# Two recurrent layers, 128 steps: layer 0's input product on two levels of Strassen, with its PSUM banks lent from layer to layer

## The chip, the core and the metric

The kernel runs on one core of one Trainium2 chip. A core has five engines, each with a queue of its own that it works off in order: TensorE (PE: matmuls, and PEld, its weight loads, which overlap them), VectorE (DVE), ScalarE (ACT), GpSimd (POOL) and SyncE (SP, which here only issues DMAs). Matmul results go to PSUM, 8 banks of 128 partitions x 512 float32. The metric is the time of one execution on the device in microseconds (us), lower is better.

## The reference

Two recurrences over the 128 steps of x (batch 128, 128 steps, 512 features), all in float32, with the same initial state:

```
step0(h, z_t):  gate = sigmoid(h @ Wh.T + z_t @ Wz.T + b);  h' = tanh(h * (1 - alpha) + gate * z_t)
x = x + layer0(x)                 # all hidden states of layer 0
step1(h, xw_t): h' = tanh(xw_t + h @ Wh1),   xw = x @ Wx1 + b1
x = x + layer1(x)                 # result, 128 x 128 x 512
```

Per step and layer there are two products of 128 x 512 by 512 x 512: the **state product** with the last state, which is bound to the order of the steps, and the **input product**, which isn't and is made for several steps at once.

## The kernel before

All data lie with the features on the partitions: a step's x is a tile of 128 x 4 x 128 (feature within a block, feature block, batch). Steps go in groups of G = 4. `prepare_x` (VectorE, L151) transposes a loaded x into the group's tile T (`ring`); a residual add on POOL (L353) puts each layer's state into it in place; `finish` (VectorE, L156, then four stores on SP) transposes it back for the output. Each step has two residual adds per layer, one for each half of the features.

**State product** (L295): 16 matmuls of 128 columns, in two halves of two feature blocks, each half with a PSUM bank of its own, ps0 and ps1 (suffix a for layer 0, b for layer 1). A matmul is two records in the profile. Before it, the bank is seeded with the step's part of the input product by a ScalarE copy (L288), onto which the matmuls accumulate. Layer 0's gate (L338), mix (L342, L344 twice) and tanh (L349) follow per half on ScalarE, VectorE, VectorE and ScalarE. Layer 1 has only the tanh (L364). For t < 4 layer 0's input product goes straight into the state's bank (L306), and the gate takes one ACTIVATE per feature block, with the bias (L336).

**Input product** (`products`, L221): one level of Strassen for a group of four steps. Input and weights are cut in 2 x 2 blocks, and 7 block products do the work of 8; a block product is 4 matmuls of 256 columns (two steps). Four of the 7 need sums of input blocks: `add_up` on POOL (L201, L206). Weight combinations are made once. Results are gathered in two PSUM banks per layer (psx and psv): products 1, 6, 7, 4 accumulate one after the other in psx, 5 and 3 in psv, and 2 in psv anew. Between two products the bank's content is kept by ScalarE (L230) or added to a kept one by VectorE (L249) into the tiles c, from which the seeds are taken. A product that accumulates in a bank therefore waits until the read before it is done. The share of a group's 7 products per step is 2, 2, 2, 1 in the order 1, 5 / 6, 3 / 7, 2 / 4, the same for both layers.

**Order.** Layer 1 runs LAG = 8 steps behind layer 0. In step t PE does layer 0's state product of t, layer 1's of t - 8, then the step's block products of both layers. The kernel writes its order out by hand: `at(due, fn, args)` puts every operation in a list with a due time, worked out from STATE = 3.57 us for a state product and PRODUCT = 1.73 us for a block product, and the list, sorted by due time, is the order in which each engine gets its instructions. Due times set the order only; at run time each engine waits for what its next instruction needs, and everything behind that waits too.

Of the kernel before, what the change touches and what calls it, by code (L numbers as in the profile page):

```python
# [13 lines left out]
def kernel(  # L14
# [31 lines left out]

    nc = tc.nc
# [8 lines left out]
    LAG = 2 * G  # L56
# [3 lines left out]
    xpool = ctx.enter_context(tc.tile_pool(name="xpool", bufs=6))  # L60
# [3 lines left out]
    cpool = ctx.enter_context(tc.tile_pool(name="cpool", bufs=2))  # L64
# [10 lines left out]
    STATE, PRODUCT = 3.57, 1.73  # L75
    def share(t):

        g, k = divmod(t, G)
        return (((), (), (), (5, 6)) if g == 0 else ((0, 1), (2, 3), (4, 5), (6,)))[k]

    start, clock = [], 24.3
    for t in range(T + LAG + 4):
        start.append(clock)
        g = t // G
        layers = (t < T) + (t >= LAG)
        groups = (g + 1 < NG) + (1 <= g <= NG)
        busy = STATE * layers + PRODUCT * len(share(t)) * groups + (STATE + 0.6 if t < G - 1 else 0.0)
        clock += max(busy, STATE + (3.0 if t < T else 0.7))
# [83 lines left out]

    class Layer:
        def __init__(self, name, bias):
            self.name, self.bias = name, bias
            self.sums, self.kept, self.bank, self.pre, self.state = {}, {}, {}, {}, {}
            self.w = const.tile([P, C, C, P], F32, tag=f"w{name}", name=f"w{name}")
            self.wh = const.tile([P, C, C, P], F32, tag=f"wh{name}", name=f"wh{name}")
            self.right = {1: self.block(0, 0), 2: self.block(1, 0), 3: self.block(1, 1)}
            for i in (4, 5, 6, 7):  # L180
                self.right[i] = const.tile([P, 2, 2, P], F32, tag=f"w{name}{i}", name=f"w{name}{i}")
# [4 lines left out]
        def combine_weights(self, i, eng):  # L186
            r, b = self.right, self.block
            one, two = {
                5: (b(0, 1), b(0, 0)), 6: (b(1, 1), r[5]), 7: (b(1, 1), b(0, 1)), 4: (b(1, 0), r[6])
            }[i]  # L190
            eng.tensor_tensor(r[i], one, two, ALU.subtract)
# [5 lines left out]
        def add_up(self, g, i):  # L197
            n, a, s = self.name, lambda i, k: self.act(g, i, k), self.sums
            s[g, i] = spool.tile([P, 2, H, P], F32, tag=f"s{n}_{i}", name=f"s{n}_{g}_{i}")
            if i == 1:  # L200
                nc.gpsimd.tensor_tensor(s[g, i], a(1, 0), a(1, 1), ALU.add)  # L201
            else:
                one, two = {
                    2: (s[g, 1], a(0, 0)), 3: (a(0, 0), a(1, 0)), 4: (a(0, 1), s.get((g, 2)))
                }[i]
                nc.gpsimd.tensor_tensor(s[g, i], one, two, ALU.subtract)  # L206

        def left(self, g, i):
            if i in (1, 2, 4):
                return self.act(g, *{1: (0, 0), 2: (0, 1), 4: (1, 1)}[i])  # L210
            return self.sums[g, {5: 1, 6: 2, 7: 3, 3: 4}[i]]

        def multiply(self, g, i, tag, first):
            if first:
                self.bank[tag] = psum.tile(
                    [P, 2, H * P], F32, tag=f"ps{tag}{self.name}", name=f"ps{tag}{self.name}_{g}_{i}"
                )
            ps, a, w = self.bank[tag], self.left(g, i), self.right[i]
            for m in range(2):
                for c in range(2):  # L220
                    nc.tensor.matmul(  # L221
                        ps[:, m], w[:, c, m, :], a[:, c],
                        start=first and m == 0 and c == 0, stop=c == 1, skip_group_check=True,
                    )

        def evacuate(self, dst, tag, half):

            for m in range(2):
                f = 2 * half + m
                nc.scalar.activation(  # L230
                    dst[:, m].rearrange("p h b -> p (h b)"), self.bank[tag][:, m], AF.Identity,
                    bias=self.bias[:, f : f + 1],
                )

        def keep(self, g, i, tag, half):
            s = spool.tile([P, 2, H, P], F32, tag=f"k{self.name}_{i}", name=f"k{self.name}_{g}_{i}")
            self.evacuate(s, tag, half)
            self.kept[i] = s

        def result(self, g, i, half):  # L240
            self.pre[g, i, half] = cpool.tile(
                [P, 2, H, P], F32, tag=f"c{self.name}_{i}{half}", name=f"c{self.name}_{g}_{i}{half}",
                bufs=1 + i,
            )
            return self.pre[g, i, half]

        def add(self, g, i, half, tag, kept):
            flat = lambda s: s.rearrange("p m h b -> p m (h b)")
            nc.vector.tensor_tensor(  # L249
                flat(self.result(g, i, half)), self.bank[tag], flat(self.kept[kept]), ALU.add  # L250
            )

        def last(self, g):
            self.evacuate(self.result(g, 1, 0), "x", 0)

        def products(self, g, places, time):

            if not 0 <= g < NG:
                return time
            order = (  # L260
                (1, "x", True, self.keep, (g, "p1", "x", 0)),
                (5, "v", True, self.keep, (g, "p5", "v", 1)),
                (6, "x", False, self.keep, (g, "u2", "x", 1)),
                (3, "v", False, self.add, (g, 0, 1, "v", "u2")),
                (7, "x", False, self.add, (g, 1, 1, "x", "p5")),
                (2, "v", True, self.add, (g, 0, 0, "v", "p1")),
                (4, "x", False, self.last, (g,)),
            )
            for place in places:
                i, tag, first, fn, args = order[place]  # L270
# [5 lines left out]
        def from_inputs(self, t, half):  # L276
            g, k = divmod(t, G)
            return self.pre[g, k // H, half][:, :, k % H]

        def state_bank(self, t, half):  # L280
            self.state[t, half] = psum.tile(
                [P, 2, P], F32, tag=f"ps{half}{self.name}", name=f"ps{half}{self.name}_{t}"
# [16 lines left out]

        def input_product(self, t):  # L300

            g, k = divmod(t, G)
            ps = [self.state_bank(t, half) for half in range(2)]
            for c in range(C):
                for m in range(C):
                    nc.tensor.matmul(  # L306
                        ps[m // 2][:, m % 2], self.w[:, c, m, :], ring[g][:, c, k],
# [3 lines left out]
    L0, L1 = Layer("a", per_feature[:, 0]), Layer("b", per_feature[:, 2])  # L311
# [16 lines left out]
    def gate0(t, i):  # L328
# [3 lines left out]
        ps = L0.state.pop((t, i))  # L332
        if t < G:
            for m in range(2):
                f = 2 * i + m
                nc.scalar.activation(s0[t][:, f], ps[:, m], AF.Sigmoid, bias=L0.bias[:, f : f + 1])  # L336
        else:
            nc.scalar.activation(s0[t][:, two[i]], ps, AF.Sigmoid)  # L338
# [40 lines left out]
    at(9.0, small_vectors)  # L379
# [9 lines left out]
    for i, time in ((1, 16.2), (2, 17.4), (4, 18.7), (3, 20.0)):  # L389
        at(time, L0.add_up, 1, i)  # L390
    L0.products(1, (0,), 14.4)
    L0.products(1, (1, 2, 3, 4), 17.4)
# [9 lines left out]
    for kc in range(C):  # L402
        at(start[2] + 6.0 + 1.5 * kc, permute_w1, L1.w, "wx", kc)
        at(start[5] + 5.0 + 1.5 * kc, permute_w1, L1.wh, "wh1", kc)
    for n, i in enumerate((5, 6, 7, 4)):
        at(start[3] + 4.5 + 1.3 * n, L1.combine_weights, i, nc.gpsimd)


    for t in range(T + LAG):
        g, k = divmod(t, G)  # L410
        now = start[t]
        if t + 3 * G < T + G and t + 2 * G < T:
            at(now + 0.01, load_x, t + 2 * G)
        if t < T:
            for i in range(2):
# [5 lines left out]
                if t + 1 >= G and t + 1 < T:  # L421
                    due = start[G] - 1.5 + 0.4 * i if t == G - 1 else end + 2.2
                    at(due, L0.seed, t + 1, i)
                at(end + 2.3, residual, t, i, h0)
            now += STATE
# [4 lines left out]
        if u >= 0:  # L430
            for i in range(2):
# [3 lines left out]
                if u + 1 < T:  # L435
                    at(end + 0.5, L1.seed, u + 1, i)
# [3 lines left out]
        now = L0.products(g + 1, share(t), now)  # L440
        now = L1.products(g - 1, share(t), now)
        if t < G:
            at((start[2] + 1.1, start[3] + 0.5, start[3] + 1.2, start[3] + 4.5)[t], prepare_x, t + LAG)
        elif t + LAG < T:
            at(0.45 * start[t] + 0.55 * start[t + 1], prepare_x, t + LAG)
        if k == G - 1:
            a, b, c = start[t + 1], start[t + 2], start[t + 3]
            for i, due0, due1 in (
                (1, a - 0.25 * (a - start[t]), max(a - 0.12 * (a - start[t]), start[t] + STATE + 2.4)),
                (2, a + 0.07 * (b - a), a + 0.2 * (b - a)),  # L450
                (4, a + 0.55 * (b - a), a + 0.65 * (b - a)),
                (3, b + 0.45 * (c - b), b + 0.55 * (c - b)),
            ):
                if g + 2 < NG:
                    at(due0, L0.add_up, g + 2, i)
                if g < NG:
                    at(due1, L1.add_up, g, i)
# [35 lines left out]
```

## Time and profile before

| | |
|---|---|
| time, median of 3 runs | 1719.63 us (1719.26 to 1719.74) |
| the profiled execution | 1719.64 us, of it the profile's span 1717.8 us |
| PE busy | 1695.2 us in 11848 matmul records |
| VectorE, ScalarE, POOL busy | 634.5, 648.4, 684.5 us |
| one group in mid-kernel (852.58 to 905.34 us) | 52.76 us, PE busy in all of it; VectorE 19.27, ScalarE 20.17, POOL 21.14 us |
| granted TensorE clock | 0.999 |
| DMA | mean 43 GB/s |

A line of the timeline has start, duration, engine, line of the kernel, operation, output<-input with a buffer's name, shapes and count; in brackets, how long the engine was idle before it and what ended that. A matmul's end is modelled, so that from the start of one run of matmuls to the start of the next is the time that it took. "Busy" of 1695.2 us is the union of the records.

### The profile page before, as it was taken

The numbers are of one execution on the slowest core, as the hardware profiler recorded it, in microseconds if no ns is written. First come the engines' busy times: TensorE is split into PE (matmuls) and PEld (weight loads), VectorE is DVE, ScalarE is ACT, GpSimd is POOL, SyncE is SP. The second block draws the span as 40 slices with busy tenths as digits, with TensorE's granted clock in tenths as the row PEclk, the third lists the DMA queues.
The fourth block names the chain that finished last, engine by engine and source line by source line (L and its number), as shares of the span: only waits on it lengthen the run. The fifth ranks groups of instructions, "written<-read, shape, count | busy, mean of one in ns | idle before, by whom it ended". The sixth has DMA issues, their size and how long they took to land.

```text
span 1717.8 us, 30477 instructions
## 1 busy us (share of the span) xinstructions
PE 1695.2 (99%) x11848; PEld 1602.1 (93%) x11848; DVE 634.5 (37%) x1234; ACT 648.4 (38%) x1792; POOL 684.5 (40%) x780
## 2 busy tenths in 40 slices
PE   6999999999999999999999999999999999999998
PEld 6899999999999999999999999999999999999998
DVE  5543333333333334333433333333333433333331
ACT  2433333433334333343333344333433333443343
POOL 2543433444334433344343344333443434444343
PEclk9999999999999999999999999999999999999999
DMA  8101112111111121111111111211111112111112
GB/s 172 38 20 43 38 38 50 38 38 43 43 40 38 38 50 38 38 44 43 39 38 42 46 38 38 46 39 40 39 42 45 38 38 45 42 38 33 24 26 50
DMA packets 153199, 73.58 MB, mean 43 GB/s; under 512 B 16801, under 2 KB 151969, under 8 KB 153057
## 3 DMA queue, kind: packets, MB, share of 16 engines
q1 hardware_dynamic: 148992, 69.53, 18.2%
q10 hardware_dynamic: 3840, 1.84, 0.6%
q8 instruction: 95, 1.56, 0.4%
q0 software_dynamic: 224, 0.27, 0.1%
q14 instruction: 48, 0.39, 0.1%
HBM read 38.02 MB, written 33.55 MB: 42 GB/s over the span
## 4 chain that ended last, share of the span: by engine, by line
PE 97%; DMA 1%; DVE 0%; ACT 0%; issue 0%; POOL 0%; ACTq 0%; POOLq 0%; DVEq 0%
PE ps0b L295 13%; PE ps0a L295 13%; PE ps1b L295 13%; PE ps1a L295 13%; PE psxb L221 13%; PE psxa L221 12%; PE psvb L221 10%; PE psva L221 9%; DMA x<-in_x_dram 1%; PE ps1a L306 0%; ACT s L336 0%; PE ps0a L306 0%; DVE s L344 0%; DVE s L342 0%; ACT h L349 0%
## 5 line engine op out<-in xcount | busy, mean ns | idle before, releaser
L353 POOL TENSOR_TENSOR T<-T,h 128x256 f32<-128x256 f32 x512 | 366.4, 726 | 1011.7 <-ACT h L349 975.0
L342 DVE TENSOR_TENSOR s<-s,T 128x256 f32<-128x256 f32 x256 | 162.7, 636 | 495.8 <-ACT s L338 479.3
L295 PEld LDWEIGHTS ps0a<-h,wha 128*128 128x128 f32 x2032 | 246.5, 192 | 8.2 <-ACT ps0a L288 1.8
L295 PE MATMUL ps0a<-h,wha 128*128 128x128 f32 x2032 | 247.4, 275 | 1.4 <-ACT ps0a L288 1.4
L295 PE MATMUL ps0b<-h,whb 128*128 128x128 f32 x2032 | 248.4, 275 | 0.1
L295 PE MATMUL ps1a<-h,wha 128*128 128x128 f32 x2032 | 247.7, 275 | 0.0
L295 PE MATMUL ps1b<-h,whb 128*128 128x128 f32 x2032 | 247.7, 275 | 0.0
L156 DVE STREAM_TRANSPOSE o<-T 128x512 f32<-128x512 f32 x128 | 91.1, 711 | 400.6 <-POOL T L353 400.6
L295 PEld LDWEIGHTS ps0b<-h,whb 128*128 128x128 f32 x2032 | 237.7, 192 | 0.9 <-ACT h L364 0.7
L295 PEld LDWEIGHTS ps1a<-h,wha 128*128 128x128 f32 x2032 | 237.1, 192 | 0.0
L295 PEld LDWEIGHTS ps1b<-h,whb 128*128 128x128 f32 x2032 | 237.1, 192 | 0.0
L349 ACT ACTIVATE h<-s 128x256 f32<-128x256 f32 x256 | 106.7, 417 | 327.4 <-DVE s L344 327.4
L338 ACT ACTIVATE s<-ps0a 128x256 f32<-128x256 f32 x124 | 47.5, 383 | 377.4 <-PE ps0a L295 377.4
L344 DVE SCALAR_TENSOR_TENSOR s<-h,leak,s 128x128 f32<-128x128 f32 x508 | 164.7, 366 | 9.0
L221 PE MATMUL psxb<-sb,wb 128*128 128x256 f32 x512 | 121.0, 379 | 0.0
L221 PE MATMUL psxb<-T,wb 128*128 128x256 f32 x512 | 121.0, 379 | 0.0
L221 PE MATMUL psvb<-sb,wb 128*128 128x256 f32 x512 | 120.9, 379 | 0.0
L221 PE MATMUL psva<-sa,wa 128*128 128x256 f32 x496 | 117.3, 379 | 0.4 <-POOL sa L201 0.4
L221 PE MATMUL psxa<-sa,wa 128*128 128x256 f32 x496 | 117.3, 379 | 0.0
L221 PE MATMUL psxa<-T,wa 128*128 128x256 f32 x496 | 117.3, 379 | 0.0
L221 PEld LDWEIGHTS psvb<-sb,wb 128*128 128x128 f32 x512 | 97.3, 190 | 13.2
L221 PEld LDWEIGHTS psxb<-sb,wb 128*128 128x128 f32 x512 | 97.0, 190 | 13.0
(78 smaller groups left out, 1758.4 us busy)
## 6 DMA issues: line engine op xcount, KB each, us to landing
out_dram<-o SPq DMA_DIRECT2D x510, 64.0 KB, 1.8
x<-in_x_dram SPq DMA_DIRECT2D x502, 64.0 KB, 2.3
wx_in<-in_L_cond_Wx_dram SPq DMA_DIRECT2D x4, 256.0 KB, 4.6
wh_in<-in_L_cond_Wh_dram SPq DMA_DIRECT2D x4, 256.0 KB, 7.1
x<-in_x_dram ACTq DMA_DIRECT2D x10, 64.0 KB, 4.1
wz_in<-in_L_cond_W_dram ACTq DMA_DIRECT2D x2, 256.0 KB, 6.5
wz_in<-in_L_cond_W_dram SPq DMA_DIRECT2D x2, 256.0 KB, 5.9
wh_in<-in_L_cond_W_dram ACTq DMA_DIRECT2D x2, 256.0 KB, 6.3
```

The lines of the kernel that those rows point to most:

```text
L156: nc.vector.transpose(dst.rearrange("p a (c j) -> p c a j", j=S), src.rearrange("p c (a i) -> p c a i", i=S))
L221: nc.tensor.matmul(ps[:, m], w[:, c, m, :], a[:, c], start=first and m == 0 and c == 0, stop=c == 1, skip_group_check=True,)
L295: nc.tensor.matmul(ps[:, m], self.wh[:, c, 2 * half + m, :], h[t - 1][:, c], start=alone and m == 0 and c == 0, stop=c == C - 1, skip_grou ...
L338: nc.scalar.activation(s0[t][:, two[i]], ps, AF.Sigmoid)
L342: nc.vector.tensor_tensor(s[:, two[i]], s[:, two[i]], at_of(t)[:, two[i]], ALU.mult)
L344: nc.vector.scalar_tensor_tensor(s[:, m], h0[t - 1][:, m], leak[:, m : m + 1], s[:, m], ALU.mult, ALU.add)
L349: nc.scalar.activation(h0[t][:, two[i]], s0[t][:, two[i]], AF.Tanh)
L353: nc.gpsimd.tensor_tensor(r, r, h[t][:, two[i]], ALU.add)
```

## The change

**Layer 0 on two levels** (`DeepLayer`). From group 2 on, each of the 7 block products is itself made by Strassen: 7 inner products of one matmul each (128 columns, one 128 x 128 weight block) for the 4 matmuls of 256 columns. 7 x 7 = 49 for 64. The 7 inner results are not combined in PSUM: they lie side by side in two banks (4 and 3), A0 and A1 or B0 and B1, and outer products accumulate onto them as before. Only after the outer combination, in SBUF, are the inner ones combined: `gather`, and then `seed_deep`, whose last addition writes the state's bank, both on VectorE. Inner sums of the inputs, 8 adds of 512 elements per group, go to VectorE (`add_up_inner`), kind 0 from x itself and kind 1 from POOL's outer sums. Inner combinations of the weights are made once on POOL. Layer 1 and group 1 of layer 0 stay on one level.

**Banks.** The four product banks belong to no layer: layer 1 uses B0, B1 and A1, layer 0 A0, A1, B0 and B1, and the steps share them out (`shares`). Layer 0's state has one tile of two banks (ra) for both halves, so that it is seeded once per step, by VectorE. Its bias comes with the gate, by one ACTIVATE per feature block at every step.

**Order.** A step now holds products of one layer only: for t = 4g layer 1's 7, 2, 4 (group g - 2); for 4g + 1 layer 0's 1, 5, 6, 3 (group g + 1); for 4g + 2 layer 0's 7, 2, 4; for 4g + 3 layer 1's 1, 5, 6, 3 (group g - 1). LAG is 9. POOL's sums of layer 0 for group g + 1 are due in step 4g, two of layer 1's in each of the two steps after it. The inner sums are due in step 4g and at the start of 4g + 1. `prepare_x` of step t + 8 is due just after `finish`. Sums stand in one tile per layer; x tiles have 5 buffers for 6, c tiles one. The small vectors are made after the first weight transposes; layer 1's weights are permuted and combined some steps later.

```diff
-    LAG = 2 * G
+    AHEAD = 2 * G
+    LAG = 2 * G + 1
-    xpool = ctx.enter_context(tc.tile_pool(name="xpool", bufs=6))
+    xpool = ctx.enter_context(tc.tile_pool(name="xpool", bufs=5))
-    cpool = ctx.enter_context(tc.tile_pool(name="cpool", bufs=2))
+    cpool = ctx.enter_context(tc.tile_pool(name="cpool", bufs=1))
...
-        return (((), (), (), (5, 6)) if g == 0 else ((0, 1), (2, 3), (4, 5), (6,)))[k]
+        said = (
+            [(1, g - 2, OUTER[4:])], [(0, g + 1, OUTER[:4])],
+            [(0, g + 1, OUTER[4:])], [(1, g - 1, OUTER[:4])],
+        )[k]
...
+        def multiply_deep(self, g, outer, tag, first):
+            for n, i in enumerate(INNER):
+                part, place = divmod(n, 4)
+                if first and place == 0:
+                    bank(f"{tag}{part}", f"{self.name}_{g}_{outer}")
+                nc.tensor.matmul(
+                    banks[f"{tag}{part}"][:, place], self.right_inner(outer, i),
+                    self.left_inner(g, outer, i),
+                    start=first and place == 0, stop=True, skip_group_check=True,
+                )
...
+        def add_deep(self, g, i, half, tag, kept):
+            c = self.part(g, i, half, half == 1)
+            k = self.kept[kept]
+            for (ps, out), (_, s) in zip(self.halves(tag, c), self.halves(tag, k)):
+                nc.vector.tensor_tensor(out, ps, s, ALU.add)
...
+        def products_deep(self, g, which, time):
+            plan_of = {
+                1: ("A", True, self.keep_deep, (g, "p1", "A")),
+                5: ("B", True, self.keep_deep, (g, "p5", "B")),
+                6: ("A", False, self.keep_deep, (g, "u2", "A")),
+                3: ("B", False, self.add_deep, (g, 0, 1, "B", "u2")),
+                7: ("A", False, self.add_deep, (g, 1, 1, "A", "p5")),
+                2: ("B", True, self.add_deep, (g, 0, 0, "B", "p1")),
+                4: ("A", False, self.last_deep, (g, "A")),
+            }
...
+        def gather(self, t, eng):
+            g, k = divmod(t, G)
+            c = self.parts[g, k // H]
+            if k % H == 0:
+                p1_p5 = c[:, :, 0:7:6]
+                eng.tensor_tensor(c[:, :, 2:4], c[:, :, 2:4], p1_p5, ALU.add)
+            else:
+                eng.tensor_tensor(c[:, :, 4], c[:, :, 4], c[:, :, 2], ALU.add)
...
+            elif k % H == 0:
+                nc.vector.tensor_tensor(out, c[:, :, 0:3:2], c[:, :, 1:4:2], ALU.add)
+            else:
+                u3 = c[:, :, 4:5].broadcast_to([P, 2, 2, P])
+                nc.vector.tensor_tensor(out, c[:, :, 5:7], u3, ALU.add)
...
-        if t < G:
-            for m in range(2):
-                f = 2 * i + m
-                nc.scalar.activation(s0[t][:, f], ps[:, m], AF.Sigmoid, bias=L0.bias[:, f : f + 1])
-        else:
-            nc.scalar.activation(s0[t][:, two[i]], ps, AF.Sigmoid)
+        for m in range(2):
+            f = 2 * i + m
+            nc.scalar.activation(
+                s0[t][:, f], L0.state[t][:, i, m], AF.Sigmoid, bias=per_feature[:, 0, f : f + 1]
+            )
...
-    at(9.0, small_vectors)
+    at(12.5, small_vectors)
...
+                if t + 1 >= 2 * G:
+                    at(now + 1.0, L0.gather, t + 1, nc.vector)
+                at(start[G] - 0.9 if t == G - 1 else end + 1.74, L0.seed_deep, t + 1)
...
-            at(0.45 * start[t] + 0.55 * start[t + 1], prepare_x, t + LAG)
+            at(max(start[t] + 2 * STATE + 1.5, 0.3 * start[t] + 0.7 * start[t + 1]), prepare_x, t + AHEAD)
-        if k == G - 1:
...
+        if k == 0 and t > 0:
+            a, b = start[t], start[t + 1]
+            at_ = lambda f: a + f * (b - a)
+            if g + 1 < NG:
+                for i, f in ((5, 0.0), (6, 0.12), (3, 0.4), (7, 0.5)):
+                    at(at_(f), L0.add_up, g + 1, i)
+                for i, f in ((5, 0.5), (6, 0.56), (3, 0.62), (7, 0.68)):
+                    at(at_(f), L0.add_up_inner, g + 1, 0, i, nc.vector)
+                for i, time in ((5, at_(0.85)), (6, at_(0.92)), (3, b + 0.01), (7, b + 0.02)):
+                    at(time, L0.add_up_inner, g + 1, 1, i, nc.vector)
+            if 0 <= g - 1 < NG:
+                for n, i in enumerate((5, 6, 3, 7)):
+                    one, after = start[t + 1 + n // 2], start[t + 2 + n // 2]
+                    at(one + (0.04, 0.55)[n % 2] * (after - one), L1.add_up, g - 1, i)
```

Unchanged in this diff, and ahead of `prepare_x` in the list: `at(end + 1.4, finish, u)`, with `end` the planned end of layer 1's state product in the step, start + 7.14 us; a block product's add or copy is due 0.05 us after the product's planned end.

## The prediction

> **What bounds it now.** I read the page's chain and busy shares first, then the timeline of one group in mid-kernel, then the first 100 us, where the kernel runs work that the rest of it lacks.
>
> ```profile
> PE 1695.2 (99%) x11848; PEld 1602.1 (93%) x11848; DVE 634.5 (37%) x1234; ACT 648.4 (38%) x1792; POOL 684.5 (40%) x780
> PE 97%; DMA 1%; DVE 0%; ACT 0%; issue 0%; POOL 0%; ACTq 0%; POOLq 0%; DVEq 0%
> ```
> TensorE is the chain, and from 100 to 847 us it is never idle; the busy times of the table by stretches agree (747.40 us busy of 747.40). So matmul time taken out counts in full, and so does every wait of PE that is put in. The timeline shows one step, the third of a group:
>
> ```profile
> 852.58 1.95 PE L295 MATMUL ps0a<-h,wha 128*128 128x128 f32 x16
> 854.37 1.95 PE L295 MATMUL ps1a<-h,wha 128*128 128x128 f32 x16
> ...
> 859.73 1.89 PE L221 MATMUL psxa<-sa,wa 128*128 128x256 f32 x8
> 861.46 1.89 PE L221 MATMUL psva<-sa,wa 128*128 128x256 f32 x8
> ...
> 862.65 0.71 POOL L353 TENSOR_TENSOR T<-T,h 128x256 f32<-128x256 f32 x1
> 863.40 0.71 DVE L156 STREAM_TRANSPOSE o<-T 128x512 f32<-128x512 f32 x1 [4.48 <-POOL T L353]
> 864.03 0.65 DVE L249 TENSOR_TENSOR ca<-psva,ka_u 128x512 f32<-128x512 f32 x1
> ```
> Starts are the measure, since PE's ends are modelled: half a state product takes 1.787 us (16 records), a block product 1.727 us (8 records of 256 columns). The reader is to see the last three lines: POOL's fourth residual add comes 10.1 us after the step's start, VectorE's output transpose waits for it, and the PSUM add behind it in VectorE's queue starts only at 11.45 us. Nothing on PE needs that add in the same step: block 7 and block 4, which share a bank with the add between them, stand in different steps.
>
> **What goes.** 30 groups' 7 block products of layer 0 become 7 inner products each: 14 records of 128 columns. At the state products' 111.7 ns per record that is 1.563 us against 1.727 us: 0.164 x 210 = **34.4 us less**. Weight loads nearly double per product, but the state products load as often and keep that pace. Layer 0's seed copies (0.376 us, 248 of them) leave ScalarE; keeping a product costs it about the same (a 128x512 COPY is 0.62 us at L168; two ACTIVATEs at L230 take 0.84). The gate goes from one ACTIVATE per half (0.38) to two (0.62 at L336). ScalarE at 38% hides all this: the last tanh of a step ends some 7 us after its start, and PE wants it after 11.8 us at the earliest. Uncovered, the gate would cost 0.24 us a half.
>
> **What comes.** VectorE gets, per group, 8 inner sums, 4 seeds, 2 gathers of 512 columns and 2 of 256, and split adds. A 128x512 add costs it 0.65 us alone (L249, L191). No row shows an add that writes PSUM, or one over blocks of 128 columns; they lie between 0.42 (256 columns, PSUM source, L362) and twice 0.65, and I take 0.6 to 0.65, the row of the same size. Its 19.3 busy us of 52.8 rise by some 11: it does not fill. What counts is the order. The order of the built program has, in the group's first step: seed, inner sums 5, 6, 3, 7, output transpose, input transpose, add of block 7 of layer 1; in its third: seed, both transposes, add of block 7 of layer 0. In both steps the products now run 7, 2, 4 back to back, and block 4 waits on that add. It has only block 2's time: 1.73 us, or 1.56 us. Behind block 4 on PE stands everything.
>
> Also moved: LAG 9 gives one more step at the end with layer 1 alone; the stores move with it and stay behind their transpose on SP's queue. There 4 stores and 4 loads take some 3.7 us a step, landing in about 2 us: hidden. One x buffer less costs nothing: a load lands some 2 us into its step and is transposed after +9. Eight weight sums more on POOL (1.27 to 1.45 us) fall at t = 1 and 2, where it shows only 0.72 us adds, and layer 1's permutes one step later on an idle ScalarE: hidden. The small vectors' 1.17 us (10.81 to 11.98) move behind the first weight transposes: the first matmul comes 0 to 1.2 us earlier, as the loads allow; I take 0.6.
>
> **The third step (t = 4g+2)**, with the step's start as 0. The two-ACTIVATE gate already stands in the trace at t = 0:
>
> ```profile
> 28.67 1.95 PE L295 MATMUL ps0a<-condT,wha 128*128 128x128 f32 x16
> ...
> 33.39 0.53 DVE L342 TENSOR_TENSOR s<-s,T 128x256 f32<-128x256 f32 x1 [1.00 <-ACT s L336]
> 33.96 0.61 DVE L344 SCALAR_TENSOR_TENSOR s<-condT,leak,s 128x128 f32<-128x128 f32 x2
> ...
> 35.10 0.72 POOL L353 TENSOR_TENSOR T<-T,h 128x256 f32<-128x256 f32 x1 [1.46 <-ACT h L349]
> ```
> POOL's second residual starts at +6.43, VectorE is free at +5.9. POOL has two more residuals (0.69 each in a row) and one sum of layer 1 (1.25) to do: its last residual ends at 6.43 + 3 x 0.70 + 1.25 = 9.8. Transposes at 0.71 and 0.63 end at 11.1, the add at 11.7; with 0.1 for the semaphore block 4 starts at 11.75. Planned: 7.15 + 2 x 1.563 = 10.25. **Wait 1.5 us.**
>
> **The first step (t = 4g).** Without any contention the same chain gives 11.85 against 7.15 + 2 x 1.727 = 10.6: 1.25 us. But POOL's two sums of layer 0 and the inner sums now fall together, and the trace shows what that does:
>
> ```profile
> 75.51 0.61 DVE L344 SCALAR_TENSOR_TENSOR s<-h,leak,s 128x128 f32<-128x128 f32 x2
> ...
> 77.40 1.45 POOL L206 TENSOR_TENSOR sa<-T 128x512 f32<-128x512 f32 x1
> 77.76 2.51 DVE L344 SCALAR_TENSOR_TENSOR s<-h,leak,s 128x128 f32<-128x128 f32 x2
> ```
> The same pair takes 2.51 us instead of 0.61 when POOL adds. At 20 to 24 us the two engines' 128x512 adds take turns, 1.67 us for one of each (POOL starts at 20.00, 21.69, 23.36; a VectorE add there lasts 1.75 us). I take turns: about 0.55 us for a VectorE 512 add, 1.12 for POOL's, 0.57 for a residual. From 4.95, POOL's sum 3 holds the gate's pair back to 6.8 (the 58.10 us pair lasted 1.50); then seed 7.4, residual 8.0, inner 5 8.5, residual 9.1, inner 6 9.65, sum 7 10.8, inner 3 11.3, residual 11.9, inner 7 12.5, transposes 13.85, add 14.5, block 4 at 14.6. **Wait 4.0 us**, between 1.25 (no contention) and 4.5 (no overlap of any op). I take the upper value, since the row with exactly these two shapes takes turns. The four later inner sums end 2 us into the next step, before its gate: free. Without that cover each would cost 0.65.
>
> **Sum.** Full groups 3 to 29: 27 x 5.5 = 148.5. Group 2, whose first step has no layer 1 state yet: 5.7 + 1.5 = 7.2. Group 30, without input transposes: 3.35 + 0.85 = 4.2. Start: t = 3 keeps one of two block products over the recurrence, 1.7; t = 4 has 5.3 us of PE work, but POOL holds back the gate's pair, so that the next state product starts near 8.1: 2.8; the first inner sums come 0.5 late at t = 5, the add 1.3 late at t = 6; one state bank of both halves at t = 0 to 2 costs 1.3 (the matmul at 33.41 waited 0.56 for one half); the small vectors give 0.6 back. Together 7.0. End: three more bare steps with 0.29 us of idle, as at 1700.55 and 1704.42: 0.9. Total +167.8. The profiled execution took 1719.64 us (span 1717.8 and 1.8 around it; median shown 1719.63): 1719.64 - 34.4 + 167.8 = 1853.0, so **1853 us**.
>
> One term is left out. After its one idle of 1.44 us (to 61.32) PE's next 16 records showed 2.05 for 1.95 us, so a restart costs 0.1. Only the first matmuls, after 13.34 us of idle, ran slow: 24 records in 5.12 us, 2.4 more than at 111.7 ns. A 4 us wait lies between: 0.1 to 2.4 us, 3 to 70 us in all over 29; nearest to it is the 1.44 us row, so 0.1, which is within the rounding. The Trainium skill, "TensorE: Matmul & The Clock Gate", section "HAM oscillation", speaks against this choice: it wants no idle above about 3.4 us, its window, or the clock halves. By its figure one window at half clock loses 1.7 us, and the sum would be some 48 us higher (an estimate). No row before has such a gap in mid-kernel.
>
> **Rivals.**
> - Turns are not strict, and the first step's wait lies nearer to 1.25 us: 28 x 2.75 = 77 less, 1776 to 1834. For it: steady steps show only L342 at 0.78 for 0.42. Against: 2.51 us.
> - The clock sinks after the long waits, or a wait that I miss adds 1 us a group: 1875 to 1924.
> - **Faster**: the adds come in time. The place is POOL's last residual in these two steps; if it ended 1.5 us earlier than 9.8, and POOL didn't hold VectorE, the transposes would be done by 9.6 and the add by 10.25. Price: only start and end remain, 1719.64 - 34.4 + 8 = 1693. It decides below (34.4 - 8) / 29 = 0.9 us of waits a group. Against: 2.75 us is the floor by rows.
> - The inner products gain nothing: if 14 records cost 123.4 ns each, 34 us more than forecast, 1887. Against: state products of the same shape.
>
> **Chances.** Forecast 1853 (1834 to 1875): 0.60; weaker contention 0.16; slow clock, further waits or no gain 0.17; faster 0.05; about even 0.02. Range 1776 to 1900 leaves out the last two and the end of the third. 0.2% (3.4 us) is about what a measurement here can tell from no change: faster 0.05, within 0.02, slower 0.93.
>
> **What would show it.** Right: PE waits at the block product lines, some 1.5 us each on an L0 add by VectorE in third steps and 4 us on an L1 add in first steps; PE busy about 1660; VectorE's output transposes waiting for POOL; inner sums lasting over 1 us. Inner products: 7 in 1.56 us. Wrong: PE gapless in mid-kernel, or gaps at a state product's start.

## The result, and the profile after

The changed kernel takes **2097.65 us** (median of 4 runs, 2096.42 to 2099.94) against 1719.68 us before in the same session: 1.220 of it, with a 95% interval of 1.218 to 1.222. The forecast was 1853 us, at most 1900. The direction was right, the size was not: the loss is 378 us where 133 were forecast. The profiled execution took 2098.06 us, its span is 2096.3 us.

The page of the changed kernel, busy times (us, share of the span, records) and the chain by engine:

```profile
PE 1796.1 (86%) x13108; PEld 1711.1 (82%) x13108; DVE 995.7 (47%) x1804; ACT 653.6 (31%) x1792; POOL 754.8 (36%) x788
...
PE 64%; DVE 13%; POOL 12%; ACT 7%; issue 3%; DMA 1%; DVEq 0%; ACTq 0%; POOLq 0%
```

TensorE was 97% of the chain and is now 64%: a third of the way to the end runs over VectorE, POOL and ScalarE. PE also became *busier* by 101 us, although 34 us of matmul work are gone. Idle time alone doesn't explain the result; the matmuls themselves ran slower, and the mean granted clock says so: 0.926 after 0.999.

PE's waits, changed kernel (engine, buffer and line waiting <- engine, buffer and line waited for: us in total, times, longest):

```profile
PE B_b L257 <- DVE cb L283: 165.7, 30, 5.7
PE A_a L392 <- DVE ca L418: 92.7, 30, 3.2
```

Both are block 4 behind the add of block 7, where the forecast had put them, but longer. The step starts in the timeline (from state product to state product of layer 0) give the account of a group; "PE's work" is the sum of its products at full clock:

| step | before | PE's work | after | wait by starts, forecast | wait by starts, after | slow matmuls |
|---|---|---|---|---|---|---|
| third, 4g+2 | 14.05 | 11.83 | 16.07 | 1.5 | 3.3 | 0.9 |
| fourth, 4g+3 | 10.60 | 14.06 | 14.85 | | | 0.8 |
| first, 4g | 14.05 | 12.33 | 20.05 | 4.0 | 5.9 | 1.9 |
| second, 4g+1 | 14.06 | 13.39 | 13.89 | | | 0.5 |
| group | 52.76 | 51.61 | 64.86 | 5.5 | 9.2 | 4.1 |

The forecast's group was 52.76 - 1.15 + 5.5 = 57.1 us; the measured one is 7.75 us longer, 3.7 of it waits and 4.1 matmuls that ran slow. Over 27 full groups that is 209 of the 245 us by which 1853 missed the profiled execution. The other 36 lie in the start, in groups 2 and 30 and at the end; at the full groups' rate the two groups have 15 of them, which leaves some 20 for the start (an estimate).

**Where the waits grew.** The timeline of a third step (start, duration, engine, line, operation, out<-in; idle before it in brackets):

```profile
993.84 3.74 PE L478 MATMUL ra<-h,wha 128*128 128x128 f32 x32
997.41 1.95 PE L326 MATMUL r0b<-h,whb 128*128 128x128 f32 x16
997.61 0.63 ACT L517 ACTIVATE s<-ra,per_feature 128x128 f32<-128x128 f32 x2 [4.66 <-PE ra L478]
...
1002.12 1.41 POOL L534 TENSOR_TENSOR T<-T,h 128x256 f32<-128x256 f32 x2 [1.46 <-ACT h L530]
...
1005.47 0.71 DVE L168 STREAM_TRANSPOSE o<-T 128x512 f32<-128x512 f32 x1 [3.27 <-POOL T L534]
...
1006.70 1.12 DVE L418 TENSOR_TENSOR ca<-A_a,ka_p 128x512 f32<-128x512 f32 x2
...
1007.40 0.71 PE L392 MATMUL A_a<-T,wca 128*128 128x128 f32 x4 [3.13 <-DVE ca L418]
```

The first half of layer 0's gate (L517) starts 3.77 us after the step, 0.2 us after the state product of *both* halves is done. Forecast was the start after the first half, 1.8 us earlier. Everything behind it comes later by as much: the second residual on POOL at +8.28 us (forecast 6.43), block 4 at +13.56 (forecast 11.75). In the first step block 4 comes at +16.47 instead of 14.6, again 1.87 later. The cover ahead of it is the same, so both waits grow by the whole delay.

**Where the matmuls slowed.** What follows the wait in that step, and the same place in the first step:

```profile
1007.40 0.71 PE L392 MATMUL A_a<-T,wca 128*128 128x128 f32 x4 [3.13 <-DVE ca L418]
...
1009.07 0.63 PE L392 MATMUL A_a<-T,wia 128*128 128x128 f32 x2
1009.50 0.63 PE L392 MATMUL A_a<-inner,wia 128*128 128x128 f32 x2
1009.93 4.51 PE L478 MATMUL ra<-h,wha 128*128 128x128 f32 x32
...
1041.22 3.78 PE L257 MATMUL B_b<-T,wcb 128*128 128x256 f32 x8 [5.70 <-DVE cb L283]
```

Block 4's 14 records start 2.53 us before the state product (1.56 at full clock), pairs of records 0.43 us apart instead of 0.22: half pace. The state product behind it takes 4.34 us by starts instead of 3.57. By the table, the waits of 3.3 and 5.9 us cost 1.7 and 2.4 us more *after* they have ended.

### The profile page after: what moved, and what is told of

The parts are those of the page before. It is cut to its first block, busy times and chain, and to the rows that moved or that the text cites. A ratio compares the mean times of both kernels' runs of the same rounds, so it can differ in the third digit from the quotient of the medians.

```text
span 2096.3 us, 33395 instructions
## 1 busy us (share of the span) xinstructions
PE 1796.1 (86%) x13108; PEld 1711.1 (82%) x13108; DVE 995.7 (47%) x1804; ACT 653.6 (31%) x1792; POOL 754.8 (36%) x788
## 4 chain that ended last, share of the span: by engine, by line
PE 64%; DVE 13%; POOL 12%; ACT 7%; issue 3%; DMA 1%; DVEq 0%; ACTq 0%; POOLq 0%
PE ra L478 23%; PE B_b L257 16%; PE A_a L392 8%; POOL T L534 8%; PE r0b L326 6%; PE r1b L326 6%; DVE s L525 5%; PE B_a L392 4%; ACT s L517 4%; DVE s L523 3%; ACT h L530 3%; POOL sa L199 2%; DVE T L163 2%; POOL sb L199 2%; DVE o L168 1%
## 5 line engine op out<-in xcount | busy, mean ns | idle before, releaser
L478 PEld LDWEIGHTS ra<-h,wha 128*128 128x128 f32 x4064 | 511.2, 206 | 17.4 <-ACT ra L468 7.2
L478 PE MATMUL ra<-h,wha 128*128 128x128 f32 x4064 | 510.8, 287 | 9.4 <-ACT ra L468 6.4
L517 ACT ACTIVATE s<-ra,per_feature 128x128 f32<-128x128 f32 x512 | 157.8, 359 | 516.4 <-PE ra L478 511.9
L257 PE MATMUL B_b<-T,wcb 128*128 128x256 f32 x256 | 115.0, 626 | 165.7 <-DVE cb L283 165.7
L326 PE MATMUL r0b<-h,whb 128*128 128x128 f32 x2032 | 249.0, 275 | 0.1
L326 PE MATMUL r1b<-h,whb 128*128 128x128 f32 x2032 | 247.7, 275 | 0.0
L326 PEld LDWEIGHTS r0b<-h,whb 128*128 128x128 f32 x2032 | 237.8, 192 | 1.3 <-ACT h L545 1.1
L326 PEld LDWEIGHTS r1b<-h,whb 128*128 128x128 f32 x2032 | 237.1, 192 | 0.0
L525 DVE SCALAR_TENSOR_TENSOR s<-h,leak,s 128x128 f32<-128x128 f32 x508 | 185.5, 407 | 9.0
L257 PE MATMUL B_b<-sb,wcb 128*128 128x256 f32 x768 | 176.5, 379 | 1.9 <-POOL T L534 1.9
L257 PEld LDWEIGHTS B_b<-sb,wcb 128*128 128x128 f32 x768 | 141.4, 190 | 22.4 <-POOL T L534 2.3
L392 PE MATMUL A_a<-inner,wia 128*128 128x128 f32 x720 | 156.6, 303 | 0.0
L392 PE MATMUL A_a<-T,wca 128*128 128x128 f32 x120 | 22.4, 311 | 92.7 <-DVE ca L418 92.7
```

Of the source, the lines that this page charges most:

```text
L257: nc.tensor.matmul(ps[:, m], w[:, c, m, :], a[:, c], start=first and m == 0 and c == 0, stop=c == 1, skip_group_check=True,)
L326: nc.tensor.matmul(ps[:, m], self.wh[:, c, 2 * half + m, :], h[t - 1][:, c], start=alone and m == 0 and c == 0, stop=c == C - 1, skip_grou ...
L392: nc.tensor.matmul(banks[f"{tag}{part}"][:, place], self.right_inner(outer, i), self.left_inner(g, outer, i), start=first and place == 0, ...
L478: nc.tensor.matmul(self.state[t][:, half, m], self.wh[:, c, 2 * half + m, :], h[t - 1][:, c], start=False, stop=c == C - 1, skip_group_che ...
L517: nc.scalar.activation(s0[t][:, f], L0.state[t][:, i, m], AF.Sigmoid, bias=per_feature[:, 0, f : f + 1])
L525: nc.vector.scalar_tensor_tensor(s[:, m], h0[t - 1][:, m], leak[:, m : m + 1], s[:, m], ALU.mult, ALU.add)
```

## The experiments

Times of one run each for e1, e2, e3 and e9; the others are medians with the 95% interval of the ratio to the kernel before.

**e1: each half of the state product in its own tile.**

```diff
-            self.state[t] = psum.tile([P, 2, 4, P], F32, tag="ra", name=f"ra_{t}")
-            return self.state[t][:, :, 0:2]
+            for i in range(2):
+                self.state[t, i] = psum.tile([P, 4, P], F32, tag=f"ra{i}", name=f"ra{i}_{t}")
+            return [self.state[t, i][:, 0:2] for i in range(2)]
```

The seed becomes two instructions, one for each tile.

> Edit: layer 0's state gets one PSUM tile per half again, each seeded by its own 128x256 add; all else as in the changed kernel. Theory A: the gate of the first half waits for the matmuls of both halves, because they share one tile, and this starts the chain gate, mix, tanh, residual, transposes, add 1.8 us later. With two tiles PE's waits at block 4 fall from 5.7 to about 4.1 us (first step of a group) and from 3.1 to about 1.5 us (third), and after the short wait the clock no longer sinks: 29 groups x (1.6 + 1.6 + 1.5) = 136 us and some 10 us at the start less than 2097.65, about 1950. If the clock sinks for another reason than the waits (theory B): waits shorter, clock the same, about 1995. If the tile does not matter: 2098.

1927.43 us, 170 less (about 1950 was expected). Its waits:

```profile
PE B_b L257 <- DVE cb L283: 110.3, 29, 3.9
PE A_a L392 <- DVE ca L418: 39.2, 30, 1.4
```

The gate starts 2.0 us into the step. The third step takes 13.45 us, a wait of 1.5 and 0.1 behind it; in the first, block 4 starts at +14.64. The forecast had 1.5 and 14.6. The rows between agree too: for the ends of the four inner sums the forecast, with VectorE and POOL taking turns, had +8.5, +9.65, +11.3 and +12.5; in the first step at 937.48 us they end at +8.66, +9.80, +11.47 and +12.59. So with the halves apart the two chains are as forecast, contention included, and the shared tile is what made them longer. A group still takes about 59.4 us against the forecast's 57.1: the first step's wait keeps its slow matmuls.

**e2: the adds of blocks 7 and 2 first.** In the first and third steps, from step 12 on, VectorE does the output's and the input's transpose and the inner sums behind the adds; tiles and all else as in the changed kernel.

```diff
-            at(end + 1.4, finish, u)
+            late = 12 <= t < T and k in (0, 2)
+            at(start[t] + 10.8 if late else end + 1.4, finish, u)
...
-                    at(at_(f), L0.add_up_inner, g + 1, 0, i, nc.vector)
+                    at(a + f2 if late0 else at_(f), L0.add_up_inner, g + 1, 0, i, nc.vector)
```

> Edit: due times only. In first and third steps VectorE's adds of blocks 7 and 2 stand ahead of the output and input transposes and (first steps) of two or four inner sums. Theory A: the waits at block 4 vanish, and the clock with them returns to 1.00; what is left is the longer start, so 1720 give or take 15. Theory B (the clock sinks because of the two-level products themselves): about 4 us a group stay, 1835. If the turns between VectorE and POOL make the wait rather than the order (theory C), a wait of over 1 us stays at block 4 in first steps and none in third steps, about 1770.

1810.79 us. First and third steps fall to 12.32 and 11.84 us, PE's work. But the second step grows from 13.39 us of work to 15.60 or 17.24: block 6 waits there for the keep of block 1 on ScalarE (L405, 58.9 us in 30 times; why, e4's timeline shows). The order alone takes 287 of the 378 us away; the expectation missed the wait that comes next.

**e3: the waits filled with matmuls that go nowhere** (22 in the first step, 11 in the third, into a bank that one bank for the state's two halves sets free), so that PE is kept busy and the waits stay.

```diff
+        if t >= 2 * G and k in (0, 2) and shares(t):
+            at(now + 2 * ((PRODUCT, DEEP)[k // 2]) - 0.01, fill, t, (22, 0, 11)[k])
```

> Edit: the order stays, but while PE waits ahead of block 4 it multiplies without use: 22 matmuls of 128 columns (4.9 us) in first steps and 11 (2.5 us) in third ones, from constant tiles into a PSUM bank that nobody reads; to free that bank, the state of layer 0 lies in one bank for two. PE does some 210 us more work. Theory A: the waits stay but no idle of over 1 us is left in them, so block 4 and the state product behind it run at full clock: 28 x 4.0 = 112 us faster than the changed kernel, about 1985. Theory B: no gain, 2098 or more.

2006.19 us, 91 less with 2046 more matmul records. Third step 15.24, first 18.32, fourth 14.06, second 13.46: exactly PE's work plus the waits of the changed kernel (3.4 and 6.0), nothing behind them, clock 0.995. Of a group's 64.86 us 3.8 were the clock. The products, their order and the waits by starts are those of the changed kernel; what differs is that PE isn't idle in them (and that the state lies in one bank for two). So the slow matmuls come with the idle time before them.

**e4: e1 and e2 together, and POOL's four sums at the start of the first step.**

```diff
-                for i, f in ((5, 0.0), (6, 0.12), (3, 0.4), (7, 0.5)):
+                for i, f in ((5, 0.0), (6, 0.01), (3, 0.02), (7, 0.03)):
                     at(at_(f), L0.add_up, g + 1, i)
```

> Edit: the two state tiles of e1, the order of e2, and POOL's sums 3 and 7 of layer 0 right behind 5 and 6, in POOL's idle time at the end of the step before. Theory A: no wait of PE left in mid-kernel; 1719.6 - 34.4 + some 10 at start and end: about 1695, faster than the kernel before by 1 to 1.5%. Theory B: still over 1800 by the sunk clock. Theory C: between, 1710 to 1760.

1743.78 us, ratio 1.014 (1.012 to 1.016): not theory A's 1695, but in the range of C. Three steps of a group are at PE's work; the second takes 14.68 for 13.39. Its timeline:

```profile
865.76 0.63 ACT L519 ACTIVATE s<-ra,per_feature 128x128 f32<-128x128 f32 x2 [0.51 <-PE ra L480]
...
868.22 0.69 DVE L199 TENSOR_TENSOR inner<-sa 128x512 f32<-128x512 f32 x1
868.82 0.69 DVE L455 TENSOR_TENSOR ca<-ca 128x512 f32<-128x512 f32 x1
869.42 0.42 DVE L525 TENSOR_TENSOR s<-s,T 128x256 f32<-128x256 f32 x1
...
870.59 0.42 ACT L532 ACTIVATE h<-s 128x256 f32<-128x256 f32 x1 [4.20 <-DVE s L527]
...
874.52 0.96 ACT L405 COPY ka_p<-A_a 128x512 f32<-128x512 f32 x2
...
875.25 0.68 PE L392 MATMUL A_a<-sa,wca 128*128 128x128 f32 x4 [1.04 <-ACT ka_p L405]
```

The gate (L519) was ready at 866.4; the mix (L525) comes at 869.42, behind four inner sums and the gather, tanh waits for it, and the keep waits in ScalarE's queue. The start phase also costs more than expected: t = 9 begins at 121.75 us (before: 113.94).

**e5: e4, with the four later inner sums behind the mixes of the second step, and a mended start phase** (input products half by half, layer 1's weight combinations on VectorE, group 3's inner sums late as well, one seed and one transpose of x due later).

```diff
-                for i, time in ((5, a + 10.9 if late0 else at_(0.85)), (6, a + 10.95 if late0 else at_(0.92)), (3, b + 0.01), (7, b + 0.02)):
+                for i, time in ((5, b + 2.30), (6, b + 2.31), (3, b + 4.10), (7, b + 4.11)):
...
+            order = [(c, m) for c in range(C) for m in range(C)]
+            for c, m in order if t == 0 else sorted(order, key=lambda p: p[1] // 2):
...
-        at(start[5] + 1.3 * n, L1.combine_weights, i, nc.gpsimd)
+        at(start[5] + 7.0 + 0.1 * n, L1.combine_weights, i, nc.vector)
...
-                late0 = g > 2
+                late0 = g > 1
```

> Theory (order of the queues and the shared state tile): in the run with split state tiles, early GpSimd sums and late inner sums, only the second step of a group stayed long (14.68 us for 13.39 us of PE's work), since VectorE did the inner sums of the sums ahead of the mix. Here those four follow the mixes of that step (two after each half), and in the start phase the input products go half by half, layer 1's weight combinations move from GpSimd to VectorE, and group 3's inner sums follow the add of block 7 as in the later groups. Expected: second step 13.4 to 13.6 us, a group 51.6 to 51.9 us (before: 52.76), t=9 at 108 to 116 us, in all 1700 us (1690 to 1715), that is 0.98 to 0.997 of before. Rival (the product on two levels can't win here, a wait only moves on): block 5 of the second step now waits for the inner sums, or the step behind it for the mix, by 1 us or more: 1725 us or more.

**1703.64 us, ratio 0.991 (0.989 to 0.993): 0.9% faster than the kernel before.** A group takes 51.62 us, steps 11.84, 14.05, 12.33 and 13.40. Its page:

```profile
PE 1668.7 (98%) x13108; PEld 1616.2 (95%) x13108; DVE 990.6 (58%) x1928; ACT 668.7 (39%) x1796; POOL 721.5 (42%) x784
...
PE 93%; DVE 3%; DMA 1%; ACT 1%; POOL 1%; issue 1%; SPq 0%; POOLq 0%; DVEq 0%; ACTq 0%
```

The same 13108 records as in the changed kernel, 127 us less busy, and TensorE is the chain again. VectorE is busy within 1% of before (990.6 us for 995.7); what differs is the order of the queues, the tiles and the start phase.

**e6: POOL's early sums alone** (the edit of e4 on the changed kernel).

> The changed kernel with one edit: GpSimd makes all four sums of a group at the start of the group's first step, where two of them lay beside VectorE's inner sums. Theory (the wait is queue order; the port costs a part): the inner sums and the product at L525 ahead of the add fall to their undisturbed 0.68 and 0.42 us, which takes about 2 us of the 5.70 us wait of the first step and nothing of the third step's: 27 x 2 = 54 us, about 2040 us (2015 to 2065). Rival (turns at the port make most of the wait): under 2 us are left of it, and with it the slow products go: 1985 us or less.

2035.18 us (1.184; 1.182 to 1.186), 62 less. The first step's waits fall from 165.7 to 105.3 us, 2.0 each, the third's stay at 92.7. The time is as expected, the reason only in part. Of VectorE's rows, the mix beside the moved sums falls from 1.50 to 0.61 us, but three of the four inner sums still last 1.10, 1.09 and 1.20 us beside POOL's residuals and its sum for layer 1 (first step at 1000.00 us; 0.68 alone). So 2.0 us is what the two moved sums cost, of the 2.75 us that the forecast's turns gave to all contention (4.0 - 1.25); the turns with the residuals are still in the wait that is left, beside queue order and the tile.

**e7 and e8: the adds first in the first step alone, and in the third alone** (e2 with `k in (0,)` or `(2,)`).

> The changed kernel with one edit: from step 12 on, in the first step of a group alone, the four inner sums, the output's and the input's transposes stand behind the add of block 7 on VectorE. Theory: the first step falls from 20.05 to about 12.3 us, the second step grows by 1.5 to 3.5 us as it did where both steps were mended, the third stays at 16.1: 4.2 to 6.2 us a group, 1930 to 1985 us. Rival (the clock sinks for another reason than the wait): only the 5.7 us go, the first step keeps slow products and takes 14 us or more.

> The changed kernel with one edit: in the third step of a group alone the output's and the input's transposes stand behind the add of block 2 on VectorE. Theory: the third step falls from 16.07 to about 11.85 us, the fourth from 14.85 to 14.06 us, since the first products behind the wait no longer run slow; the first step's 5.7 us wait stays: 5.0 us x 27 = 135 us, 1963 us (1945 to 1990). Rival (the clock sinks for another reason): the third step keeps slow products, 13.5 us or more, and the gain is under 90 us.

1948.33 us (1.134; 1.132 to 1.136) and 1959.38 us (1.140; 1.138 to 1.141). In e7 the first step takes 12.33 us, the second 15.6 to 17.4; in e8 the third 11.84 and the fourth 14.06. The gains, 149 and 138 us, add up to e2's 287: the two waits are independent, and each takes its slow matmuls with it.

**e9: a ramp of waits.** e5 with n copies of 128x128 by VectorE ahead of block 7's add, n growing by one from group to group.

```diff
+    def hold(t):
+        spare = const.tile([P, P], F32, tag="spare", name=f"spare_{t}")
+        for _ in range(t // G - 3):
+            nc.vector.tensor_copy(spare, banks["A0"][:, 0])
```

> The mended kernel (e5) with a ramp: in the third step of group g, VectorE makes g - 3 copies of 128x128 of the bank with block 7's products (they go nowhere) ahead of the add of block 7, so that TensorE waits at block 4 by nothing in group 4 and by some 4 to 6 us in group 30, in steps of about 0.2 us. Of each wait the time that the 48 records behind it lose is read. Theory (the loss is a step): about 0.1 us behind every wait up to some 1.8 us, about 1.7 us behind every wait from some 2.3 us on, no more behind 5 us than behind 3. Rival 1 (proportional): it grows with the wait, about 0.4 us for each us. Rival 2 (the Trainium skill, TensorE: Matmul & The Clock Gate, HAM oscillation: the clock halves after idle of more than about 3.4 us): 0.1 us up to waits of 3.4 us. In all 1703.6 plus waits of 40 to 80 us plus, by the theory, 1.7 x 14 to 18: 1770 to 1815 us.

1824.44 us, somewhat above the expectation (waits up to 7.2 us). What block 4 and the state product behind each wait, 46 records, lost against full pace:

| wait, us | lost behind it, us |
|---|---|
| 0.37, 0.70, 1.02, 1.35, 1.67 | 0.1 each |
| 2.00, 2.33, 2.65, 2.98 | 1.7, 1.6, 0.1, 0.1 |
| 3.30, 3.62, 3.95, 4.27, 4.60, 4.92 | 1.7, 2.6, 2.5, 1.7, 2.2, 1.7 |
| 5.25, 5.58, 5.90, 6.22, 6.55, 6.87, 7.20 | 3.1, 1.9, 2.8, 1.5, 2.3, 2.5, 2.5 |

Two of these waits in the timeline, 1.67 and 5.25 us, each with the state product behind it:

```profile
718.09 0.71 PE L392 MATMUL A_a<-T,wca 128*128 128x128 f32 x4 [1.67 <-DVE ca L418]
...
719.75 3.74 PE L480 MATMUL ra<-h,wha 128*128 128x128 f32 x32
...
1343.60 1.22 PE L392 MATMUL A_a<-T,wca 128*128 128x128 f32 x4 [5.25 <-DVE ca L418]
...
1346.75 5.20 PE L480 MATMUL ra<-h,wha 128*128 128x128 f32 x32
```

It is a step and not a slope: 0.1 us up to 1.67 us, 0.1 or 1.7 between 2 and 3, from 3.30 on 1.5 to 3.1 and 2.2 on average (13 waits). A proportional loss is refuted. The Trainium skill, "TensorE: Matmul & The Clock Gate", section "HAM oscillation", wants no idle above about 3.4 us and has, in its example, some 1.67 us of slow time behind each wait; here the waits above 3.4 us all cost the clock too, but those of 2.00 and 2.33 us lost 1.6 to 1.7 us as well, and the half clock stood for 3.41 us, 6.83 us or once 10.24 us.

What decides between 2 and 3 us is the place of the wait in time, and the granted clock in the profile shows it. A line has a stretch in us, its length, the busy time (and records) of PE, PEld, VectorE, ScalarE and POOL, the granted clock, and the DMA's share and GB/s:

```profile
769.55:772.97 3.42, 1.42 (x13) 1.23 (x13) 3.25 (x10) 0.00 (x0) 0.00 (x0) 1.00 0.00 0
772.97:776.38 3.41, 3.41 (x19) 3.41 (x18) 2.25 (x5) 1.06 (x2) 0.00 (x0) 0.50 0.31 63
...
933.40:936.81 3.41, 2.33 (x21) 2.13 (x20) 2.94 (x11) 0.03 (x1) 1.71 (x2) 1.00 0.00 0
936.81:940.23 3.42, 1.53 (x13) 1.53 (x14) 3.32 (x9) 0.33 (x1) 0.00 (x0) 1.00 0.00 0
940.23:943.64 3.41, 3.41 (x33) 3.41 (x32) 2.32 (x5) 1.35 (x4) 0.00 (x0) 1.00 0.31 61
```

In each profile of the changed kernel and of e1 to e11, the granted clock changes between 1.00 and 0.50 only at points a whole number of 3.413 us apart (to 3 ns): time falls into slots of that length. The wait of 2.00 us (769.97 to 771.97) lies whole in one slot, and the next slot runs at half clock. The wait of 2.98 us (935.73 to 938.70) is cut by a slot's end into 1.08 and 1.89 us, and no half clock follows. The waits of 2.33 us (2.11 and 0.22) and 2.65 us (1.00 and 1.65) go the same two ways.

The other runs say the same. After the start phase (from 190 us on) the changed kernel and e1 to e11 hold 269 waits of PE of over 1.5 us. Of 41 with less than 1.9 us in any one slot, none was followed by half clock; of 189 with over 2.05 us in one slot, all were; in between it was 33 of 39. In e2 the second step's wait is nearly always 1.97 us: 12 of 28 lie whole in a slot and cost 1.7 us each, the other 16 leave at most 1.71 us in a slot and cost 0.1. In e7 9 of 27 waits of 3.13 us lost only 0.1, cut by a slot's end near their middle. A slot at half clock in which PE is busy throughout loses 1.7 us, half of its length; two of them, less what of them is still the wait, give the losses up to 3.1.

**e10: e5 with one level** (layer 0's blocks as plain block products; no inner sums, gathers or VectorE seeds).

```diff
-            elif group == 1:
+            elif group >= 1:
                 now = L0.products(group, which, now)
```

> The mended kernel (e5) with layer 0's blocks as plain block products (49 block products become 56): no inner products, inner sums or gathers, the seeds copied by ScalarE; all else of e5 stays, the order of the queues and the banks. What two levels are worth by themselves, by the forecast's own row: 210 x 0.164 = 34.4 us. Theory: a group takes 52.76 us as before the change, less up to 9 us of waits in the start phase, in all 1733 us (1722 to 1742). Rival (e5's gain over the kernel before comes from the order and the banks, not from the products): 1710 us or less.

1727.87 us (1.005; 1.003 to 1.007), a group 52.76 us. In the same order and banks, two levels are worth 24.2 us: 27 x 1.14 = 31 in full groups, less what the start phase gives back (t = 5, for one, takes 15.7 us in e5 and 12.2 here). The order and the banks by themselves cost 8 us, so e5's gain comes from the products.

**e11: e5 with the shared tile back.**

> The mended kernel (e5) with one edit undone: the two halves of a state product share one tile again, so that the gate of the first half waits for the second half. Theory: the gate, the mixes and the inner sums behind them come 1.8 us later; in the second step block 5 then waits for the last inner sums by 0.3 to 1.5 us, the other steps are covered since the adds stand ahead of the transposes; in the start phase waits come back: 1733 us (1712 to 1770). Rival (the shared tile is harmless once the adds come first): 1710 us or less.

1746.5 us (1.016; 1.014 to 1.017). The second step takes 14.06 us, 0.67 more than its work, for 18 us in all; most of the rest of the 43 us comes in the start phase: t = 14 begins 21.9 us later than in e5. Size and place were as expected, the wait is not: block 6 waits for the keep of block 1 (L405, 10.7 us in 27 times, one of them 2.5 us in the start phase), not block 5 for the inner sums.

## Why the prediction was right in direction and wrong in size

- **Bound by TensorE; every wait counts in full:** right. e5 removes the waits and stands at PE's work.
- **34.4 us less by 49 products for 64:** right for full groups. 14 records take 1.56 us, a group of e5 is 1.14 us shorter than before (1.15 forecast); over the whole kernel, start included, the comparison of e5 with e10 gives 24.2 us. "PE busy about 1660": 1668.7 in e5, 1796.1 in the changed kernel, since slow matmuls count as busy.
- **"Third step: wait 1.5 us":** the first step that failed. The forecast read the start of the gate off a row of the kernel before (28.67 us) whose two halves had a bank each, and took over its "second residual at +6.43". With one tile for both halves the gate waits for the whole state product. Measured +8.28 and a wait of 3.3. The text had named the shared bank only for t = 0 to 2. Undone in e1, the wait is 1.5.
- **"First step: wait 4.0 us":** the same fault, 5.9 measured; block 4 at +14.64 in e1 against 14.6 forecast. The strict turns of VectorE and POOL, the disputed choice, held row by row (e1), so that the 14.6 was no luck.
- **"One term is left out", 0.1 us per wait:** the second that failed, and the larger one (4.1 of the 7.75 us). The nearest row was a wait of 1.44 us, and e9 shows that it lies on the other side of a step. Where the forecast's own 4.0 us wait stands, in e1, a group takes 2.3 us more than forecast (59.4 for 57.1), so with every other number right the sum would still have been low by some 2.3 x 29 = 67 us (an estimate). The longer third wait came over the bound too (e1: 0.1 behind 1.5 us; changed kernel: 1.7 behind 3.3). The page's rule, for which the forecast gave +48, was nearer than the row chosen.
- **"Together 7.0" for the start:** too low by about 20 us. t = 4 begins 8.9 us after the time of before: the input products of t = 1 to 3 wait 2.8 to 2.9 us each, the whole tile again ("costs 1.3" in the forecast), and at t = 5 the step takes 17.4 us for 10.5. There the mix of the first half takes 2.51 us instead of 0.61 beside layer 1's weight sums on POOL, the keep of block 1 stands behind it on ScalarE, and block 6 waits 3.25 us for that. The clock has a part here too: between 35 and 97 us PE is busy for 16.1 us at half clock (none in the kernel before), which is 8 us lost. "Eight weight sums more on POOL ... hidden" held, but only because the gate came late: in e4, with the halves apart, the mix at t = 1 and 2 runs beside them and takes 1.50 us instead of 0.61.
- **"The four later inner sums are free":** true only while the step before them was long. In e2 and e4 they held back the mix.
- **Rivals.** "The clock sinks, or a wait that I miss adds 1 us a group" named both causes, and had 1 us where they took 7.75. "Faster: the adds come in time, 1693": not this kernel, but e5 brings the adds in time by order alone and comes to 1703.6.

What stays open: the exact bound on idle time in a slot (between 1.9 and 2.05 us, 33 of 39 waits cost the clock), and how the 20 us of the start divide.

## What to carry to other kernels

When an edit puts two results into one tile, follow the *first* consumer of the first result: it now waits for the second, and the whole chain behind it moves, here by 1.8 us in each of two waits. A wait of the matmul engine has a second price that begins only where it ends: none below some 1.9 us; from there to 3.5 us it depends on whether some 2 us of the wait fall into one slot of 3.41 us; every wait of over 3.5 us in these runs paid it, 1.5 to 3.1 us each in e9, whatever its length. So shortening a wait below the bound is worth more than the wait. When a queue is reordered to serve one wait, look at once for what now stands last in it: the cheap fix of e2 made a new wait one step on, and only the version that put each operation just ahead of its own consumer (e5) got the gain of the products.

## What was not expected of the hardware

The loss behind a wait does not grow with it: 2.6 us behind 3.62 us of idle, 1.5 behind 6.22. It goes by slots: about 2 us of idle within one slot of 3.41 us and the next one runs at half clock, so that the same 1.97 us wait cost 1.7 or 0.1 us from group to group (e2). While it lasts, records come 0.214 us apart instead of 0.112. And idle time can be bought off: 2046 matmuls that compute nothing made the changed kernel 91 us faster (e3).
